# New duration constants for the planner of a decoder layer with a selective scan and a routed mixture of experts

## The chip, the cores and the metric

The kernel runs on one core of a Trainium2 chip. The metric is device time in microseconds. The core has five engines that work side by side, each taking its own instructions strictly in the order in which the program holds them: TensorE (PE, matmuls), VectorE (DVE), ScalarE (ACT), GpSimd (POOL) and SyncE (SP), which here only issues DMA transfers.

## What is computed

One decoder layer on x of shape 4 x 512 x 512 (batch, positions, width): a state-space block with a scan over positions, a quantized two-layer product in place of cross attention, and a mixture of 16 experts of which each token takes two, beside a shared expert. Cut to what matters:

```python
x = x + attn(layernorm(x))      # the scan block
x = x + xattn(layernorm(x), fside, ctx)
x = x + ffn(layernorm(x))

# attn: xz = in_proj(h); x = silu(conv1d(x)); dt, Bc, Cc = x_proj(x)
# delta = softplus(dt_proj(dt) + bias); A = -exp(A_log)
def step(h, inputs):
    d_t, B_t, C_t, u_t = inputs
    h = h * exp(d_t * A) + (d_t * u_t) * B_t      # 1024 channels x 16 states
    return h, (h * C_t).sum(states)
# y = (ys + u * D) * silu(z); out_proj(y)

# xattn: int8-like: both operands scaled by column and row maxima, rounded
#        to -127..127, multiplied, scaled back; silu(gate) * up between two such
# ffn:   softmax routing, top 2 of 16 experts (width 128), weighted sum,
#        plus sigmoid(x @ g) * shared expert (width 512)
```

## The kernel before

The scan runs on VectorE for one batch element b after the other, and in it for eight channel blocks c of 128 channels (NC = 8). A channel block takes eight slots (NU = 8), so that there are 4 x 8 x 8 = 256 slots. In a slot (`scan_batch`) ScalarE computes two exponentials `da` of 128 x 512 for the next slot (`unit_inputs`, L709) and GpSimd the product `bu` (L711); VectorE runs the scan of 128 x 1024 in place on `da` (`unit_scan`, L718) and multiplies the result by C into `h` (`unit_out`, L724), of which there are five buffers. Twice in eight slots PE sums the states of four such `h` into the PSUM tile `py` (`state_sums`, L736: 16 quarter-array matmuls for the eight slots), and VectorE multiplies the sum by the gate (`gated`, L758).

Everything else is placed beside these slots, in pieces called steps. Each kind of work is a Python generator that yields what its next step waits for:

- `delta(b, c)`: the step size of channel block c, one matmul, five ACT operations with one change of table, four POOL operations; its result is replicated by DMA (`spread`, tile `rep`) and feeds `da` and `bu`. It is wanted one channel block later; if it is late, `end` forces its steps out.
- `front(b)`, b = 1 to 3: layernorm, 64 matmuls of in_proj (L446, four of 512 columns to a product), convolution, gate, x_proj.
- `back(b)`: out_proj (L791), two quantized products, and the mixture's front: routing and the shared expert. Backs 0 to 2 run beside the scans of the next batch; the last comes after the scans.
- `experts` for group 0 (batches 0 and 1; beside the last scan batch) and group 1 (batches 2 and 3; after the scans): sorting of the tokens, then tiles of 128 tokens with weights fetched by an indirect DMA (L1223), tokens by another (L1467), transposes, the products L1498 and L1513, and at the end the fetch and weighted sum of the rows (L1261, L1271).

What places a step is `Pace`, an estimate of when each engine is free and each tile written. For each instruction already in the program, `take` adds a cost to its engine's clock: a fixed part (FIXED) and a part per element (EACH) for DVE, ACT and POOL, a product of columns for PE (`product`), and a fixed part for a DMA issue. A written tile is ready for others HOP = 120 ns after that. Nothing of this runs on the chip; it decides only the order in which instructions stand in each engine's program.

Three times in a slot `more` asks the waiting steps in turn, and `clear` says yes if every engine of the step is at most BEHIND past VectorE's clock (0 DVE, 1500 ACT, 500 POOL, 5000 PE, 4000 SP, in ns) and its inputs are ready at most SLACK past it (200 DVE, 700 ACT, -300 POOL, 3500 PE, 500 SP). For engines other than DVE the slot's own coming work (3500, 1200 or 0 ns, by the place in the slot) is added. Steps behind a planned count (`due`) are given 100 ns more for each step that they are late. After the scans `run` takes the step that the estimate has ready first.

The three PSUM banks bank_a, bank_b and bank_g serve all steps beside the scan; after it there are five more.

Of the kernel before, what the change touches and what calls it, by code (L numbers as in the profile page):

```python
# [8 lines left out]
F32 = mybir.dt.float32  # L9
# [21 lines left out]
CH = 32  # L31
# [15 lines left out]
PE, ACT, POOL, SP = "PE", "Activation", "Pool", "SP"  # L47
# [15 lines left out]
class Bank:  # L63
# [9 lines left out]
    def take(self, shape, dtype=F32):  # L73
        pool, name = self.names.pop(0)
        t = pool.tile(shape, dtype, name=name, tag=name, bufs=1)
        self.held[name_of(t)] = pool, name
        return t
# [7 lines left out]
    def staged(self, items, product, *stages, freed=1):  # L85

        gap = [nothing] * (self.depth - freed)
        return staged(items, product, *gap, *stages, every=1 if gap or self.depth == freed else freed, bank=self)
# [44 lines left out]
class Pace:  # L133

    FIXED = {"DVE": 60, "Activation": 220, "Pool": 130, "PE": 30, "SP": 60}
    EACH = {"DVE": 1.1, "Activation": 0.92, "Pool": 2.2}
    HOP = 120
    TABLES = {"Exp": 0, "Tanh": 0, "Silu": 1, "Ln": 2}  # L140

# [4 lines left out]
    def __init__(self, nc):  # L146
        self.nc, self.seen, self.table, self.queue = nc, 0, None, 0
        self.rest = 0
        self.engine = dict.fromkeys(self.FIXED, 0)
        self.written, self.read = {}, {}  # L150
# [6 lines left out]
    def take(self, ins):  # L157
        outs = [x for x in ins.outs if hasattr(x, "bass_ap")]
        ins_ = [x for x in ins.ins if hasattr(x, "bass_ap")]
        e = str(ins.engine).rsplit(".", 1)[-1]  # L160
        if not outs or e not in self.engine:
            return
        n = 1
        for _, size in list(outs[0].ap)[1:]:
            n *= size
        kind = type(ins).__name__
        keys, outs_ = [self.key(x) for x in ins_], [self.key(x) for x in outs]
        start = max([self.engine[e]] + [self.written.get(k, 0) for k in keys])
        if e != "SP":
            start = max([start] + [max(self.written.get(k, 0), self.read.get(k, 0)) for k in outs_])  # L170
        if "DMA" in kind:
            end = start + (950 if e == "Pool" else self.FIXED[e])
            size = 1
            for _, x in outs[0].ap:
                size *= x
            self.queue = max(self.queue, end) + size * 4 / 220
            self.engine[e], done = end, max(self.queue, end + 1000) + 1000
        else:
            if e == "PE":
                cost = 40 + self.product(n / 4 if outs[0].ap[0][1] == CH else n, ins_[0].dtype == F32)  # L180
            else:
                cost = self.FIXED[e] + n * self.EACH[e] * (2 if getattr(ins, "is_tensor_tensor_scan", False) else 1)
            if e == "Activation" and kind == "InstActivation":
                table = self.TABLES.get(str(ins.func).rsplit(".", 1)[-1], self.table)
                if table != self.table:
                    cost += 1280
                    self.table = table
            self.engine[e] = start + cost
            done = self.engine[e] + self.HOP
        for k in keys:  # L190
            self.read[k] = max(self.read.get(k, 0), done)
        for k in outs_:
            self.written[k] = done

    def product(self, cols, full):

        return max(2.3 * cols, 300) if full else max(0.5 * cols, 120)

    def update(self):
        ins = self.nc.cur_bb.bb.instructions  # L200
# [69 lines left out]
class Kernel:  # L270
# [271 lines left out]
    def first_front(self, sb, bank):  # L542
# [54 lines left out]
        for _ in staged(range(NC), product, conv, silu, nothing, sums):  # L597
            pass
# [1168 lines left out]
```

## Time and profile before

| | us |
|---|---|
| median of 3 runs | 1646.77 (1646.59 to 1649.17) |
| the profiled execution | 1661.86 |
| its span, first to last instruction | 1659.9 |
| scan stages, about | 90 to 1335 |
| idle of ACT before da, for h | 229.4 |
| idle of POOL before bu, for da | 140.2 |
| longest wait of VectorE for bu | 27.4 |

The profile is one execution taken by the hardware profiler. A row of the groups gives source line, engine and operation, output and inputs with shapes, the count, then busy us in all and the mean ns of one, then the idle time of the engine just before and what ended it. ACT's and POOL's long waits above are for buffers that VectorE gives back: these engines are ahead of it there. An fp32 matmul leaves two records on PE, so counts of matmuls there are twice the program's.

The time of PE depends on the clock that it is granted. The page gives it in forty slices of the span, in tenths of full speed:

```
PEclk9978888768877887899978897987777999868995
```

### The profile page before, as it was taken

How to read it: one execution, taken by the hardware profiler on the slowest of the kernel's cores; microseconds unless marked ns; L12 is line 12 of the kernel's file. 1: busy time of each engine (PE TensorE's matmuls, PEld its weight loads, DVE VectorE, ACT ScalarE, POOL GpSimd, SP SyncE). 2: the span in 40 equal slices, each digit the busy share in tenths (PEclk: the TensorE clock that was granted, in tenths of full speed). 3: DMA queues.
4: the chain of work that ended last, by engine and by line, in shares of the span. 5: the costliest groups of instructions: out<-in, count | busy, mean ns of one | idle time of the engine just before them, and what ended most of it. 6: DMA issues, size and time to landing. Idle time of an engine off the chain costs nothing. (4 is left out here: it accounts for less than half of the span.)

```text
span 1659.9 us, 15722 instructions
## 1 busy us (share of the span) xinstructions
PE 1207.7 (73%) x4552; PEld 584.8 (35%) x4552; DVE 1193.2 (72%) x1250; ACT 941.3 (57%) x1592; POOL 1130.7 (68%) x940
## 2 busy tenths in 40 slices
PE   6848777557866767898867885866667899668980
PEld 2213222112332323333423432343424347434760
DVE  4369999898867888778878898877778934352312
ACT  3376786755757778555787762567575414520330
POOL 1178999886767988676787874777788644126464
PEclk9978888768877887899978897987777999868995
DMA  5575655675233556665335658555567464168956
GB/s 192 154 162 126 141 110 111 130 189 110 74 90 78 135 120 163 161 203 143 78 84 127 172 137 293 138 158 133 130 184 204 120 260 146 65 230 292 342 213 216
DMA packets 109658, 262.22 MB, mean 158 GB/s; under 512 B 16192, under 2 KB 20416, under 8 KB 109504
## 3 DMA queue, kind: packets, MB, share of 16 engines
q1 hardware_dynamic: 93120, 204.50, 47.4%
q0 software_dynamic: 16448, 56.65, 9.8%
q8 instruction: 40, 0.66, 0.2%
q14 instruction: 50, 0.41, 0.1%
HBM read 168.55 MB, written 45.88 MB: 129 GB/s over the span
## 5 line engine op out<-in xcount | busy, mean ns | idle before, releaser
L711 POOL TENSOR_TENSOR bu<-bc,rep 128x1024 f32<-128x1024 f32 x256 | 602.2, 2358 | 169.8 <-DVE da L718 140.2
L718 DVE TENSOR_TENSOR_SCAN da<-da,bu 128x1024 f32<-128x1024 f32 x256 | 586.2, 2290 | 105.2 <-POOL bu L711 74.4
L709 ACT ACTIVATE da<-rep,a_sb 128x512 f32<-128x512 f32 x512 | 352.7, 690 | 261.2 <-DVE h L724 229.4
L724 DVE TENSOR_TENSOR h<-da,bc 128x1024 f32<-128x1024 f32 x256 | 312.3, 1220 | 19.6 <-PE py L736 9.2
L736 PE MATMUL py<-h,sel 128*32 128x512 f32 x1024 | 166.1, 687 | 50.2 <-DVE h L724 50.1
L1223 POOL DMA_INDIRECT wx<-in_wexp,wrow x62 | 63.0, 1016 | 79.9 <-PE bank L1513 22.9
L446 PE MATMUL bank_g<-xnT,win 128*128 128x512 f32 x192 | 100.2, 670 | 8.6 <-ACT tap L498 6.0
L502 POOL TENSOR_TENSOR u<-u,tap 128x511 f32<-128x511 f32 (+2 forms) x72 | 91.3, 1268 | 18.1 <-ACT tap L498 15.9
L446 PE MATMUL bank_b<-xnT,win 128*128 128x512 f32 x160 | 82.1, 661 | 24.6 <-ACT sp_r L669 15.2
L736 PEld LDWEIGHTS py<-h,sel 128*32 128x32 f32 x1024 | 31.1, 119 | 164.4 <-issue 83.3
L1467 POOL DMA_INDIRECT xs<-xn_d,tok x62 | 64.3, 1038 | 20.9 <-issue 19.2
L446 PE MATMUL bank_a<-xnT,win 128*128 128x512 f32 x128 | 63.2, 640 | 3.0 <-DVE gz L411 2.4
L446 PEld LDWEIGHTS bank_g<-xnT,win 128*128 128x128 f32 x192 | 40.5, 219 | 63.0 <-issue 51.2
L446 PEld LDWEIGHTS bank_b<-xnT,win 128*128 128x128 f32 x160 | 32.9, 213 | 72.9 <-issue 38.5
L680 POOL TENSOR_TENSOR sp_e<-sp_e,dd 128x512 f32<-128x512 f32 x32 | 40.7, 1272 | 26.2 <-ACT dd L675 26.1
L1261 POOL DMA_INDIRECT yg<-y_d,pos x32 | 33.3, 1041 | 23.9 <-DMA y_d<-ys 9.5
L1504 ACT ACTIVATE hs<-bank 128x128 f32<-128x128 f32 x24 | 6.6, 276 | 67.5 <-PE bank L1498 36.5
L1271 DVE SCALAR_TENSOR_TENSOR xr<-yg,topw,xr 128x512 f32<-128x512 f32 x32 | 23.7, 750 | 28.8 <-DMA yg<-y_d,pos 28.5
L791 PE MATMUL bank_b<-wout,u 128*128 128x512 f32 x64 | 36.1, 724 | 10.7 <-ACT tap L498 6.2
L1498 PE MATMUL bank<-xT,wx 128*128 128x128 f32 x352 | 43.1, 276 | 0.6 <-issue 0.6
L1498 PEld LDWEIGHTS bank<-xT,wx 128*128 128x128 f32 x352 | 41.3, 192 | 4.3 <-issue 3.5
L411 DVE SCALAR_TENSOR_TENSOR hs<-hs,bank 128x128 f32<-128x128 f32 x24 | 6.8, 284 | 50.1 <-ACT hs L1504 35.7
(422 smaller groups left out, 2439.4 us busy)
## 6 DMA issues: line engine op xcount, KB each, us to landing
rep<-dd SPq DMA_DIRECT2D x128, 512.0 KB
win<-in_win SPq DMA_DIRECT2D x64, 256.0 KB
x<-xr SPq DMA_DIRECT2D x48, 256.0 KB
xr<-x SPq DMA_DIRECT2D x48, 256.0 KB
y_d<-ys SPq DMA_DIRECT2D x48, 256.0 KB
bc<-rows_d SPq DMA_DIRECT2D x32, 256.0 KB
gz_d<-gz SPq DMA_DIRECT2D x32, 256.0 KB
gzl<-gz_d SPq DMA_DIRECT2D x32, 256.0 KB
```

Of the source, the lines that this page charges most:

```text
L446: nc.tensor.matmul(pj, win[:, k, :], xnT[:, k, :], start=(k == 0), stop=(k == NK - 1))
L502: nc.gpsimd.tensor_add(u[:, j:], u[:, j:], v[j][:, j:])
L680: nc.gpsimd.tensor_sub(e, e, du)
L709: nc.scalar.activation(da[:, i, :], rep[:, i, 0, :], AF.Exp, scale=self.a_sb[:, q, g : g + 1])
L711: nc.gpsimd.tensor_mul(bu, st["bc"][0, g].unsqueeze(1).to_broadcast([P, NP, L]), rep[:, :, 1, :])
L718: self.nc.vector.tensor_tensor_scan(daf, daf, buf, 0.0, ALU.mult, ALU.add)
L724: self.nc.vector.tensor_mul(h, st["da"].pop((c, n)), st["bc"][1, g].unsqueeze(1).to_broadcast([P, NP, L]))
L736: nc.tensor.matmul(py[q * CH : (q + 1) * CH, :], self.sel, st["h"][c, g, q // NP][:, q % NP, :], start=False, stop=(g == NG - 1),)
L791: nc.tensor.matmul(po[t], st["u"][c][:, t * P : (t + 1) * P], wout[c], start=(c == part[0]), stop=(c == part[-1]),)
L1223: nc.gpsimd.indirect_dma_start(out=ws[s], out_offset=None, in_=self.wexp, in_offset=bass.IndirectOffsetOnAxis(ap=wrow[:, s : s + 1], axis= ...
L1467: nc.gpsimd.indirect_dma_start(out=xs[s], out_offset=None, in_=xn_d, in_offset=bass.IndirectOffsetOnAxis(ap=tok[:, s : s + 1], axis=0), bo ...
L1498: nc.tensor.matmul(ph[:, i, :], w[:, o : o + P], xT[:, k, :], start=(k == 0), stop=(k == NK - 1))
```

## The change

The constants of the estimate are replaced: those of VectorE, ScalarE, GpSimd and PE, the cost of a GpSimd DMA issue, and the 40 ns that were added to each matmul. HOP, the table load, the DMA queue's rate, SLACK, BEHIND and the due times stay as they are. The diff:

```diff
-    FIXED = {"DVE": 60, "Activation": 220, "Pool": 130, "PE": 30, "SP": 60}
-    EACH = {"DVE": 1.1, "Activation": 0.92, "Pool": 2.2}
+    FIXED = {"DVE": 150, "Activation": 190, "Pool": 180, "PE": 0, "SP": 60}
+    EACH = {"DVE": 1.044, "Activation": 0.9, "Pool": 2.13}
     HOP = 120
...
         if "DMA" in kind:
-            end = start + (950 if e == "Pool" else self.FIXED[e])
+            end = start + (1030 if e == "Pool" else self.FIXED[e])
...
             if e == "PE":
-                cost = 40 + self.product(n / 4 if outs[0].ap[0][1] == CH else n, ins_[0].dtype == F32)
+                cost = self.product(n / 4 if outs[0].ap[0][1] == CH else n, ins_[0].dtype == F32)
...
     def product(self, cols, full):
-        return max(2.3 * cols, 300) if full else max(0.5 * cols, 120)
+        return max(1.8 * cols, 240) if full else max(0.6 * cols, 110)
```

`full` is true for fp32 operands. `n / 4` is used for the state sums, whose four quarter-array matmuls of 32 output rows count as 128 columns each. For scans the part per element counts twice.

## The prediction

> **What bounds the kernel now.** I read the page's busy shares first, then busy time by stage, then the costliest groups, then the waits of VectorE, and the timeline where a number had to be taken apart.
>
> ```profile
> PE 1207.7 (73%) x4552; PEld 584.8 (35%) x4552; DVE 1193.2 (72%) x1250; ACT 941.3 (57%) x1592; POOL 1130.7 (68%) x940
> ```
>
> No engine is full over the span. The stages say more (columns: stretch, its length, then busy us of PE, weight loads, DVE, ACT, POOL, granted clock, DMA share, GB/s):
>
> ```profile
> 90.00:360.00 270.00, 184.75 (x536) 62.18 (x536) 244.26 (x164) 196.37 (x310) 238.93 (x168) 0.82 0.59 128
> 360.00:670.00 310.00, 218.85 (x776) 99.33 (x776) 252.73 (x226) 221.08 (x372) 246.59 (x198) 0.82 0.50 121
> 670.00:1000.00 330.00, 272.45 (x920) 119.68 (x919) 273.91 (x252) 218.16 (x360) 251.62 (x188) 0.89 0.55 138
> 1000.00:1335.00 335.00, 232.83 (x996) 122.75 (x995) 273.57 (x290) 187.61 (x323) 237.40 (x198) 0.82 0.59 167
> 1335.00:1660.00 325.00, 237.58 (x1197) 157.26 (x1195) 112.93 (x275) 88.44 (x187) 143.55 (x161) 0.85 0.63 224
> ```
>
> From 90 to 1335 us the scan runs, 256 slots of it. VectorE is the backbone: 244.3 of 270 us in the first batch (90%), then 252.7 of 310, 273.9 of 330 and 273.6 of 335 (82% together). The sum of its idle time there is 1245 - 1044.5 = 200.5 us. Behind the scan lie 325 us in which PE is the busiest at 73%. A slot's own work:
>
> ```profile
> L711 POOL TENSOR_TENSOR bu<-bc,rep 128x1024 f32<-128x1024 f32 x256 | 602.2, 2358 | 169.8 <-DVE da L718 140.2
> L718 DVE TENSOR_TENSOR_SCAN da<-da,bu 128x1024 f32<-128x1024 f32 x256 | 586.2, 2290 | 105.2 <-POOL bu L711 74.4
> L709 ACT ACTIVATE da<-rep,a_sb 128x512 f32<-128x512 f32 x512 | 352.7, 690 | 261.2 <-DVE h L724 229.4
> L724 DVE TENSOR_TENSOR h<-da,bc 128x1024 f32<-128x1024 f32 x256 | 312.3, 1220 | 19.6 <-PE py L736 9.2
> ```
>
> VectorE needs 2290 + 1220 = 3510 ns a slot; measured is 1245 / 256 = 4.86 us. The difference is the work placed beside the scan and the idle time. Who is waited for by VectorE from 90 to 1335 us (total us, times, longest):
>
> ```profile
> DVE da L718 <- POOL bu L711: 74.4, 29, 27.4
> DVE da L718 <- ACT da L709: 29.4, 17, 4.4
> DVE u L758 <- PE py L736: 12.2, 4, 8.5
> DVE h L724 <- PE py L736: 9.2, 3, 5.3
> ```
>
> 41.0 us of the first line fall before 360, the 27.4 at the scan's start. The waits on PE are few.
>
> **The change, part by part.** No instruction is added or removed. The constants only move the planner's clocks, and with them the place of each step. So the cost is the order's cost, bounded from the estimates' errors.
>
> *VectorE and GpSimd.* By the formula a scan goes from 60 + 2.2 x 1024 = 2313 to 2288 (row 2290), h from 1186 to 1219 (row 1220), bu from 2383 to 2361 (row 2358). A slot's VectorE estimate goes from 3499 to 3507 ns: nothing. GpSimd's own DMA issues go from 950 to 1030 ns (rows 1016 to 1041): 28 issues beside the scan (62 + 62 in all, 48 + 48 of them after 1335) x 80 ns = 2.2 us of estimate, nothing. SP's constant stays; its issues move with their steps, and SP mostly waits for their data, so no queue there is costlier.
>
> *ScalarE.* 512 elements go from 691 to 651 ns; the row of da says 690, while small copies take 620 to 680. Two da a slot become 80 ns cheaper in the plan than their row. Since da waits for h in each slot, the error does not add up: 0 to +0.1 us a slot on the few slots where ACT is last (17 waits): at most 2 us.
>
> *PE.* This is the change. A 512-column fp32 matmul goes from 40 + 1178 = 1218 to 922 ns; a 128-column one, and each of the state sums' quarter-array ones, from 340 to 240. The load that the planner sees for eight slots of the middle batches: state sums 16 x 340, one skip and one delta matmul: 7.9 us, now 5.7; a front's ten 512-column matmuls 12.2, now 9.2; an eighth of a back (80 of 512 columns, 168 of 128, some bf16) 20.7, now 15.5. Sum 40.8 before, 30.4 after. Measured, eight slots take (1000 - 360) / 128 x 8 = 40 us. So the old planner held PE for full, and spread its steps; the new one sees it at three quarters, and admits them sooner. Real matmuls:
>
> ```profile
> 548.98 6.68 PE L446 MATMUL bank_g<-xnT,win 128*128 128x512 f32 x8 [5.41 <-ACT tap L498]
> 557.71 1.92 PE L736 MATMUL py<-h,sel 128*32 128x512 f32 x16
> 559.56 3.70 PE L446 MATMUL bank_b<-xnT,win 128*128 128x512 f32 x8
> ```
>
> Eight records are one product of four matmuls (each fp32 matmul leaves two). After a pause of 5.41 us it takes 6.68 us, warm 3.70: 1.67 and 0.925 us a matmul. The new constant is the warm one. **A rule against it**: the Trainium skill ("TensorE: Matmul & The Clock Gate", Part 1) says the array drops to half clock after an idle window of about 3.4 us and needs as long a busy one to recover. The row agrees: 6.68 against 3.70, and the granted clock of the scan is 0.82 to 0.89, which is a third of its time at half: (1 - 0.84) / 0.5. Weighted so, a matmul is 0.67 x 0.925 + 0.33 x 1.67 = 1.17 us at worst, my estimate, or 922 / 0.84 = 1.10. By the old constant the plan is 4 to 11% long; by the new, 16 to 21% short. By the rule's mean the eight-slot load would be 30.4 / 0.84 = 36 us, between the two.
>
> What does that cost? The planner admits a PE step while PE's clock is under 5 us (plus up to 3.5) past VectorE's; these tolerances stay. Behind an admitted product stand, on PE's in-order queue, the state sums, and behind these the five h buffers and the py bank that VectorE needs next. The sums are issued at the start of a slot and the first h buffer is wanted some 1.7 slots later, 1.7 x 4.86 = 8 us. A backlog planned at 5 us is on the mean 4.5 to 4.8 today and 6.0 to 6.3 with the new constants; with the 3.5 us besides, about 10, past the cover. Batches 1 to 3 hold 24 x 2 = 48 state sums; a third fall in half clock, 16. Bounds: 0 (the cover holds, as for 45 of 48 today) to 16 x 3 us = 48. I take 8, near today's rows (9.2 + 12.2), since steps rarely fill the tolerance.
>
> Besides, VectorE's small operations that read PE's result are placed once the plan has it ready (200 ns slack). Some 46 a back (4 out_proj sums, 22 in the two quantized products, the rest in the mixture's front) and 3 a channel block: 3 x 46 + 24 x 3 = 210. Each now goes up to 0.3 us earlier (1218 - 922) for each matmul before it; where it was waited for anyway nothing is lost. Bounds: -10 (results truly ready that were left lying) to 210 x 0.3 = 63; I take 14, a third of them at 0.2.
>
> *What it gives.* Steps once held for PE go sooner. A place where that was late:
>
> ```profile
> 472.40 2.30 DVE L718 TENSOR_TENSOR_SCAN da<-da,bu 128x1024 f32<-128x1024 f32 x1 [11.64 <-POOL bu L711]
> 474.60 0.67 DVE L411 SCALAR_TENSOR_TENSOR u<-bank_b,u 128x512 f32<-128x512 f32 x1
> 475.19 0.68 DVE L951 TENSOR_REDUCE wsc<-bank_a 128x1 f32<-128x512 f32 x1
> ```
>
> There the delta of the next block came late, its spread was still landing, and VectorE stood 11.64 us. Such waits for POOL and ACT between 360 and 1335 sum to 103.8 - 41.0 - 5.0 = 58 us (5.0 is ACT's share before 360). Bounds 0 to -58; I take -12, one such stall.
>
> *A second rule.* The two last lines start 0.59 us apart, though each lasts 0.67. "Perfetto Trace Analysis" (Optimizing Scalar/DVE Operations) says why: a profiled duration holds a write acknowledgement that the next instruction overlaps. The old formula gave 60 + 563 = 623 for this shape, the new 684. By the row's spacing the old one is nearer: 420 such operations (932 of VectorE in the scan stages less 512) x 0.08 = 34 us of invented VectorE time, 2.7% of 1245. It makes the plan's "now" late and so the other engines' tolerances looser: the same direction, inside the bounds above.
>
> *Behind the scan* the step that is ready first by the estimate is taken. The order of the last back and the tiles can move, by an amount no row tells: -10 to +10 (3% of 325), 0 taken.
>
> Sum: +8 + 14 - 12 + 0 = **+10 us**. The profiled execution took 1661.9 us (span 1659.9 and 2.0 around it), 0.9% above the median of 1646.8; differences of 10 us need no scaling. Forecast **1657 us**.
>
> **The rivals.**
>
> *Faster: POOL and ACT are no longer booked into time that does not exist.* A plan bound by PE (40.8 us and its waits) stretches its own clock, so that VectorE, POOL and ACT seem to have room; with PE right, it spaces their steps by the real period. For it: where PE was light, in the first batch, VectorE was 90% busy. Half of the 58 us goes: -29. And the tail shrinks: expert tiles leave 16 records each on L1498, 736 in all and 528 after 1335, so 46 tiles, 13 of them beside the scan and, with 23 a group, 10 of the first left over. Three more moved, at about 3.8 us of PE, times PE's 73%: -8. It gives 1647 - 37 = 1610. It decides once the plan admits the late deltas' steps without queueing over the sums. Against it: the waits are scattered, and the first batch has no backs.
>
> *Much slower: chains fall behind in slots.* A shorter planned slot means that a step waiting for ACT or POOL becomes ready more slots later; fewer tiles run beside the scan, and the due-time term forces late steps onto busy queues. Five tiles fewer: +19, and the forecast's +10: 1676. Against it: PE's part of the chains shortens too.
>
> *No effect*: forced points (late deltas, due steps) decide the order, or the gains cancel: 1647.
>
> **How the numbers follow.** Forecast 0.44 (own range 1650 to 1668), faster 0.36, much slower 0.13, no effect 0.07. Within 0.2% is about what a measurement of this kernel can tell from no change (3.3 us). Faster 0.36, same 0.07, slower 0.57. The range runs from 1598 (-58 and a few tiles cut by a third) to 1700 (+48 + 14 less the gain): both signs hold most of the chance.
>
> **What would show it.** Right: waits of h and of the gating (L758) on PE py rise above 21 us, the small readers' waits on PE grow, POOL waits fall a little, the scan still ends near 1335 to 1350. Wrong: the scan's VectorE share rises above 86% with PE waits unchanged (rival one), or more than 33 tiles behind the scan (rival two). An unchanged order of the engines would undo all of it.

## The result, and the profile after

The changed kernel takes **1674.4 us** (four runs, 1673.0 to 1676.0) against 1646.8 before: ratio 1.0166, with a 95% interval of 1.0144 to 1.0189. That is 28 us slower. The direction was forecast and the time lies in the stated range, but the forecast was +10 us.

The one profiled execution that the prediction was worked from took 1661.9 us, 15 us above the median of its kernel. The same program profiled again (run e1_before_again) gave 1642.9 us of span and 1646.9 us median; it stands for "before" in what follows. Busy shares after, from the page:

```profile
PE 1208.3 (72%) x4552; PEld 590.7 (35%) x4552; DVE 1195.7 (71%) x1250; ACT 943.3 (56%) x1592; POOL 1128.9 (67%) x940
```

The work is the same. Busy time by stage, first for the kernel before (profiled again), then for the changed one. The stages run from the first scan to the first scan of the next batch, the fourth to the last scan, the fifth to the end; columns as in the prediction.

```profile
89.40:350.20 260.80, 176.79 (x524) 59.49 (x524) 237.82 (x159) 192.95 (x304) 234.86 (x166) 0.81 0.59 128
350.20:667.50 317.30, 224.45 (x788) 99.65 (x788) 260.85 (x233) 225.33 (x379) 252.29 (x202) 0.83 0.51 124
667.50:991.30 323.80, 267.34 (x914) 118.26 (x915) 270.53 (x249) 216.11 (x358) 249.11 (x186) 0.90 0.55 138
991.30:1328.50 337.20, 234.93 (x999) 127.56 (x998) 275.06 (x290) 188.46 (x324) 238.59 (x199) 0.81 0.59 167
1328.50:1642.90 314.40, 237.63 (x1197) 160.03 (x1195) 113.54 (x275) 89.16 (x187) 144.05 (x161) 0.83 0.65 232
```

```profile
89.70:363.50 273.80, 188.69 (x524) 62.09 (x524) 239.33 (x160) 192.58 (x304) 234.60 (x166) 0.76 0.55 121
363.50:676.30 312.80, 239.28 (x836) 107.34 (x840) 264.19 (x239) 225.87 (x381) 253.33 (x202) 0.85 0.54 132
676.30:1013.10 336.80, 263.00 (x898) 116.84 (x892) 269.88 (x247) 214.35 (x354) 245.58 (x185) 0.89 0.51 130
1013.10:1374.80 361.70, 253.19 (x1129) 144.82 (x1126) 280.17 (x302) 195.01 (x340) 248.97 (x209) 0.84 0.61 176
1374.80:1673.30 298.50, 205.12 (x1041) 136.90 (x1039) 106.71 (x260) 85.32 (x172) 133.06 (x151) 0.83 0.61 216
```

The second column is what to read. The scan lasts 1239.1 us before and 1285.1 after: +13.0, -4.5, +13.0 and +24.5 by batch, +46 in all. Behind it 314.4 became 298.5: -16. The sum is the +30 between the two profiles.

VectorE's longest waits from the first to the last scan, before (again) and after, with us, times and longest:

```profile
DVE da L718 <- POOL bu L711: 73.9, 28, 27.2
DVE da L718 <- ACT da L709: 29.1, 17, 4.4
DVE u L758 <- PE py L736: 10.7, 5, 6.9
DVE h L724 <- PE py L736: 6.3, 2, 4.5
DVE xsc L1005 <- PE bank_b L940: 6.2, 5, 2.5
```

```profile
DVE da L718 <- POOL bu L711: 61.6, 23, 27.3
DVE da L718 <- ACT da L709: 41.6, 27, 5.2
DVE xn L1122 <- PE bank_b L1099: 17.4, 6, 7.0
DVE xn L1122 <- PE bank_a L1099: 11.0, 5, 4.7
DVE xsc L1005 <- PE bank_a L940: 10.9, 5, 8.5
DVE h L724 <- PE py L736: 10.7, 5, 3.9
```

L1122, the shared expert's product read from PSUM, stands in the second list with 28.4 us; before it was 5.4. Summed over all lines and batches, VectorE's waits went from 208 to 245 us: on PE 67 to 97, on ACT 47 to 65, on POOL 93 to 78, on a DMA 0 to 5. It was also busy 9 us longer there (1044.3 to 1053.6), since more steps stand beside the scan. 37 + 9 = 46.

How such a wait looks, in the changed kernel's last batch, first VectorE, then PE:

```profile
1310.49 2.29 DVE L718 TENSOR_TENSOR_SCAN da<-da,bu 128x1024 f32<-128x1024 f32 x1
1317.49 0.69 DVE L1122 SCALAR_TENSOR_TENSOR xn<-xn,bank_a 128x512 f32<-128x512 f32 x1 [4.71 <-PE bank_a L1099]
1318.10 0.68 DVE L411 SCALAR_TENSOR_TENSOR xn<-xn,bank_b 128x512 f32<-128x512 f32 x1
1318.70 1.22 DVE L724 TENSOR_TENSOR h<-da,bc 128x1024 f32<-128x1024 f32 x1
```

```profile
1309.91 3.67 PE L1107 MATMUL bank_b<-xnT,ws 128*128 128x512 f32 x8 [3.27 <-DMA ws<-in_wexp]
1313.42 0.60 PE L400 MATMUL bank_g<-ident,xs 128*128 128x128 f32 x4
1313.86 3.60 PE L1099 MATMUL bank_a<-xnT,ws 128*128 128x512 f32 x8
```

The scan ends at 1312.8. VectorE's order has L1122 next; PE had waited 3.27 us for weights and finishes its product at 1317.5. Behind L1122 stands the h that ends the slot, though its own input is there. So the larger part of this wait came with the weights' DMA; in all, PE waited 18 us for these weights (tile ws) during the scan, 11 before. From the 241st scan to the last it is 89.1 us here and 69.6 before.

### The profile page after: what moved, and what is told of

It reads as the page before. It is cut to its first block, busy times and chain, and to the rows that moved or that the text cites. A ratio compares the mean times of both kernels' runs of the same rounds, so it can differ in the third digit from the quotient of the medians.

```text
span 1673.3 us, 15705 instructions
## 1 busy us (share of the span) xinstructions
PE 1208.3 (72%) x4552; PEld 590.7 (35%) x4552; DVE 1195.7 (71%) x1250; ACT 943.3 (56%) x1592; POOL 1128.9 (67%) x940
## 5 line engine op out<-in xcount | busy, mean ns | idle before, releaser
L724 DVE TENSOR_TENSOR h<-da,bc 128x1024 f32<-128x1024 f32 x256 | 312.5, 1221 | 21.5 <-PE py L736 10.7
L736 PEld LDWEIGHTS py<-h,sel 128*32 128x32 f32 x1024 | 30.2, 115 | 200.4 <-DVE h L724 127.7
L446 PE MATMUL bank_a<-xnT,win 128*128 128x512 f32 x168 | 91.3, 694 | 2.9 <-DVE gz L411 1.1
L446 PE MATMUL bank_g<-xnT,win 128*128 128x512 f32 x152 | 75.5, 643 | 2.6 <-ACT tap L498 1.9
L446 PEld LDWEIGHTS bank_a<-xnT,win 128*128 128x128 f32 x168 | 36.9, 228 | 54.5 <-issue 46.2
L446 PEld LDWEIGHTS bank_g<-xnT,win 128*128 128x128 f32 x152 | 30.8, 208 | 46.3 <-issue 38.6
L1498 PE MATMUL bank_g<-xT,wx 128*128 128x128 f32 x208 | 32.3, 321 | 13.3 <-ACT xT L1489 7.3
L684 POOL TENSOR_TENSOR dd<-sp_e,sp_w 128x512 f32<-128x512 f32 x32 | 40.6, 1267 | 1.6 <-ACT sp_w L678 0.6
L686 POOL TENSOR_TENSOR dd<-dd,u 128x512 f32<-128x512 f32 x32 | 40.6, 1270 | 1.4
L682 POOL TENSOR_TENSOR sp_e<-sp_e,sp_r 128x512 f32<-128x512 f32 x32 | 40.6, 1269 | 1.4
```

The source lines that it names most:

```text
L446: nc.tensor.matmul(pj, win[:, k, :], xnT[:, k, :], start=(k == 0), stop=(k == NK - 1))
L682: nc.gpsimd.tensor_add(e, e, r)
L724: self.nc.vector.tensor_mul(h, st["da"].pop((c, n)), st["bc"][1, g].unsqueeze(1).to_broadcast([P, NP, L]))
L736: nc.tensor.matmul(py[q * CH : (q + 1) * CH, :], self.sel, st["h"][c, g, q // NP][:, q % NP, :], start=False, stop=(g == NG - 1),)
```

## The experiments

Each is timed against the kernel before, side by side on the same chip, and shown as a ratio with its interval. "Scan" is the time from the first scan to the last, "three" the part of it that the first three batches take, "behind" what follows the last scan, "PE" VectorE's waits on PE during the scan, "tiles" the expert tiles begun beside it, all from the run's own profile.

| run | ratio | scan, us | three, us | behind, us | PE, us | tiles |
|---|---|---|---|---|---|---|
| e1_before_again | 1.0002 [0.9989, 1.0015] | 1239 | 902 | 314 | 67 | 13 |
| the change | 1.0166 [1.0144, 1.0189] | 1285 | 923 | 298 | 97 | 18 |
| e1_pe_only | 1.0201 [1.0176, 1.0226] | 1295 | 941 | 297 | 105 | 17 |
| e1_rest_only | 0.9917 [0.9899, 0.9934] | 1236 | 901 | 309 | 63 | 15 |
| e1_hop125 | 1.0029 [1.0011, 1.0046] | 1249 | 910 | 314 | 87 | 13 |
| e2_tol | 1.0160 [1.0126, 1.0195] | 1288 | 921 | 304 | 107 | 17 |
| e2_new_to_192 | 1.0099 [1.0077, 1.0120] | 1242 | 917 | 339 | 73 | 10 |
| e2_new_from_192 | 1.0198 [1.0173, 1.0223] | 1287 | 906 | 314 | 106 | 19 |
| e2_hold | 1.0232 [1.0205, 1.0259] | 1273 | 920 | 329 | 94 | 13 |
| e3_late | 0.9975 [0.9956, 0.9995] | 1245 | 905 | 325 | 68 | 15 |
| e3_early | 1.0362 [1.0327, 1.0397] | 1317 | 962 | 317 | 116 | 17 |
| e3_mean | 1.0238 [1.0202, 1.0273] | 1300 | 952 | 310 | 116 | 18 |
| e3_slow | 1.0365 [1.0329, 1.0400] | 1257 | 922 | 372 | 64 | 12 |
| e4_margin | 1.0086 [1.0053, 1.0119] | 1288 | 932 | 299 | 124 | 17 |
| e4_after_hop115 | 1.0343 [1.0303, 1.0384] | 1320 | 942 | 311 | 154 | 17 |
| e4_rest_hop115 | 1.0033 [1.0017, 1.0049] | 1245 | 909 | 328 | 79 | 14 |
| e4_rest_plus | 1.0171 [1.0128, 1.0215] | 1245 | 908 | 356 | 75 | 14 |
| e5_large_old | 1.0119 [1.0088, 1.0149] | 1282 | 929 | 290 | 104 | 17 |
| e5_small_old | 0.9882 [0.9854, 0.9909] | 1254 | 928 | 287 | 106 | 13 |

**Which half of the change?** Before with one half of the constants, with nothing, and with another signal time.

> The kernel before, unedited, profiled once more. Every theory expects 1646 to 1650 us timed. Its first profile was 15 us above its own median; if that was one odd execution, this profile's run is within 5 us of 1647, and the stages that lengthened can be read from its windows. If profiled executions of this kernel are long as such, it is near 1660 again.

> The kernel before with only PE's constants of the change (no 40 ns, 1.8 ns a column with a floor of 240, 0.6 with a floor of 110). Theory 1, PE is overbooked beside the scan: nearly the whole loss is here, 1667 to 1680 us, with more than 13 expert tiles beside the last scan batch and the last scan after 1355. Theory 2, any re-ordering of this plan costs: slower too, but no more than the other half of the constants, 1655 to 1665. Rival, PE's true durations help and the others hurt: at or below 1640.

```diff
-                cost = 40 + self.product(...)
+                cost = self.product(...)
-        return max(2.3 * cols, 300) if full else max(0.5 * cols, 120)
+        return max(1.8 * cols, 240) if full else max(0.6 * cols, 110)
```

> The kernel before with the change's constants of VectorE, ScalarE and GpSimd, and PE's old ones. Theory 1: within 8 us of 1647. Theory 2 (any re-ordering costs): 1655 to 1680, as much as PE's half. Rival, the others hurt: 1665 or more.

```diff
-    FIXED = {"DVE": 60, "Activation": 220, "Pool": 130, "PE": 30, "SP": 60}
-    EACH = {"DVE": 1.1, "Activation": 0.92, "Pool": 2.2}
+    FIXED = {"DVE": 150, "Activation": 190, "Pool": 180, "PE": 0, "SP": 60}
+    EACH = {"DVE": 1.044, "Activation": 0.9, "Pool": 2.13}
-            end = start + (950 if e == "Pool" else self.FIXED[e])
+            end = start + (1030 if e == "Pool" else self.FIXED[e])
```

> The kernel before with the estimate's signal time at 125 ns in place of 120: an order as different as chance makes it, with no duration truer or falser. Theory 1: within 8 us of 1647. Theory 2: 1655 to 1680, like the change.

```diff
-    HOP = 120
+    HOP = 125
```

PE's half alone gives 1.0201, as much as the whole within the intervals; the other half 0.9917, a gain. The loss is PE's. "Any re-ordering costs" is not borne out: an order changed by nothing but 5 ns of signal time gives 1.0029, the other half's a gain.

**Is it the tolerance, the batch, or the work pulled in?** These are edits of the changed kernel.

> The changed kernel with PE's two tolerances cut by the ratio of the constants, 922/1218 = 0.76: BEHIND 5000 to 3800, SLACK 3500 to 2650 ns. If the loss is a backlog admitted by tolerances that stayed in nanoseconds (the prediction's step), the time falls to 1635 to 1655. If it is the length of the plan, PE's load being taken for three quarters of what it is, whatever the tolerance, it stays at 1665 to 1685.

```diff
-    SLACK = {..., "PE": 3500, ...}
-    BEHIND = {..., "PE": 5000, ...}
+    SLACK = {..., "PE": 2650, ...}
+    BEHIND = {..., "PE": 3800, ...}
```

> The changed kernel's constants up to slot 192 (fronts, backs 0 and 1), then the old ones for the last scan batch and behind it. If the loss is spread over all batches: 1655 to 1665. If it comes from the last batch, where expert tiles and the last back's out_proj enter beside the scan: 1640 to 1652.

> The reverse: the old constants up to slot 192, the change's from there. Spread loss: 1655 to 1665. Loss of the last batch: 1665 to 1680, the whole of it.

```diff
+            if self.slot == 192:
+                self.pace.use(False)
```

(`use` puts all constants of the change, or all the old ones, in force. The second run begins with the old ones and has `use(True)` here.)

> The changed kernel with two kinds of work kept behind the scan: no expert tile after the 13th begins beside it, and the last back's out_proj waits for its end. Theory, work pulled beside the scan lengthens it while behind it that work was hidden by the last back's chain: last scan before 1350 and 1640 to 1660 us. If the loss lies in how the other steps stand: 1670 or more.

```diff
-            while started < loaded and len(going) < bank.depth:
+            while started < loaded and len(going) < bank.depth and (started < 13 or "scans" in self.done):
...
-                    yield PE, *wout, lambda: ("gated", b, part[-1]) in self.done
+                    yield PE, *wout, lambda: ("gated", b, part[-1]) in self.done and "scans" in self.done
...
+            if not going:
+                yield lambda: "scans" in self.done
+                continue
...
         self.finish(B - 1, 1)
+        self.done.add("scans")
```

The tolerance, the prediction's own mechanism for the queue, is not borne out: with it cut in proportion the ratio stays at 1.016. The two halves in time give 1.0099 and 1.0198; they don't add up to 1.0166, but neither is free, so the loss isn't the last batch's alone. The column "three" says it more closely, since several runs have the same constants up to slot 192: with the old ones the first three batches take 902 to 908 us (e1_before_again, e2_new_from_192, and the profile that the prediction read), with the change's 917 to 923 (the change, e2_new_to_192, e2_hold).

Holding work back made it worse. Its last scan batch and what follows:

```profile
1011.70:1364.70 353.00, 234.85 (x990) 125.46 (x986) 275.88 (x290) 189.00 (x326) 240.31 (x191) 0.80 0.57 165
1364.70:1693.40 328.70, 238.68 (x1178) 160.80 (x1178) 110.90 (x272) 90.46 (x186) 142.01 (x168) 0.84 0.59 212
```

Against the change the batch is 8.7 us shorter (361.7 to 353.0) and the rest 30.2 longer (298.5 to 328.7). So the work pulled beside the scan was worth its place, and that theory falls too. From the last scan to the last routing matmul (L1157) are 143 us before and 116 after the change, where the last back's out_proj begins 18 us before the last scan and not 9 after it. The 16 us that the end gained go with this.

**PE as busy, or PE's results as ready?** Here PE's estimate is split in two clocks.

> The changed kernel with PE's estimate split in two: PE counts as busy by the new, short durations, while its results count as ready by the old, long ones. Theory R, the loss comes from results promised too early, so that their readers stand at the head of VectorE's and ScalarE's queues: the loss is gone, ratio 0.985 to 1.000. Theory Q, it comes from PE being admitted more work: ratio 1.012 to 1.022 as with the change.

> The reverse split: PE counts as busy by the old, long durations, its results as ready by the new, short ones. Theory R: the loss stays, 1.012 to 1.025. Theory Q: it is gone, 0.985 to 1.002.

```diff
+                cost = self.product(cols, full)
+                self.shadow = max(self.shadow, begin) + self.slower(cols, full)
...
-            done = self.engine[e] + self.HOP
+            done = (self.shadow if e == "PE" else self.engine[e]) + self.HOP
```

(`begin` is when the operands are ready; `slower` the old formula with its 40 ns. For e3_early the two formulas change places.)

> The changed kernel with PE's durations at what the trace gives on the mean over both clocks, 2.2 ns a column, floor 290 (bf16 0.73, floor 135), in place of 1.8 and 240. If the fault of the new constants is that they hold for the full clock alone: ratio 0.985 to 0.998. If the old ones were good for being longer than the truth: between the two, 1.003 to 1.012.

> The changed kernel with PE's durations half as long again as the change's: 2.8 ns a column, floor 380 (bf16 0.93, floor 170), above the old ones. If any slack is good: 0.985 or lower. If there is a best value near the true mean: 1.000 or more, since steps come too late and work is left behind the scan.

```diff
-        return max(1.8 * cols, 240) if full else max(0.6 * cols, 110)
+        return max(2.2 * cols, 290) if full else max(0.73 * cols, 135)    # e3_mean
+        return max(2.8 * cols, 380) if full else max(0.93 * cols, 170)    # e3_slow
```

e3_early speaks for the results: promised by the new durations, they keep the loss, and more, although PE counts as busy by the old (1.0362, waits on PE 116 us). e3_late looks like the other side of this (0.9975, 68 us) but does not test it. The planner lets a matmul wait for the promised result of the one before it on the same tile, so there PE's clock follows the long durations after all, and the plan is almost e1_rest_only's: by their traces, all but about one in a hundred of VectorE's instructions stand in the same order. (That these two give 0.9917 and 0.9975 also shows how far ratios from different groups of runs can lie apart.) e3_mean, half or more of the way back to the old durations, is worse than the change. e3_slow shows the other end: fewest waits on PE (64), a scan of 1257 us, and 372 us behind it, because the steps come too late (12 tiles).

**A margin, luck, or one kind of matmul?**

> The changed kernel, all its durations kept, with one addition: a result of PE counts as ready 1000 ns later for the readers on other engines (not for PE's own next matmul on the same tile). That is about what four matmuls lost in the change (4 x 296 ns). Theory R, the old long durations were good as a margin on PE's results: ratio 0.985 to 1.002 and VectorE's waits on PE in the scan stages fall from 97 to below 75 us. If the old durations were good for another reason, or by chance of order: 1.010 or more.

```diff
-        start = max([self.engine[e]] + [self.written.get(k, 0) for k in keys])
+        written = {**self.written, **self.own} if e == "PE" else self.written
+        start = max([self.engine[e]] + [written.get(k, 0) for k in keys])
...
         for k in outs_:
+            self.own.pop(k, None)
+            if e == "PE":
+                self.own[k] = done
-            self.written[k] = done
+            self.written[k] = done + (1000 if e == "PE" else 0)
```

(`own` holds what PE itself waits for.)

> The changed kernel with the signal time at 115 ns in place of 120: another order of the same plan. If the change's loss belongs to its durations, it stays: 1.010 to 1.025. If it is the luck of one order: anything from 0.99 to 1.03, and a value at or below 1.003 would show it.

> The new durations of VectorE, ScalarE and GpSimd with PE's old ones, and the signal time at 115 ns. If the gain of that half (0.992) belongs to its durations: 0.988 to 0.998. If it was luck: 1.000 or more.

```diff
-    HOP = 120
+    HOP = 115
```

> The same half with PE's old durations made 8% longer (2.5 ns a column, floor 325, and the 40 ns). A broad best around the old values gives 0.988 to 1.002; a best that lies in one order alone gives 1.010 or more; results that are promised later still take VectorE's waits on PE in the scan stages to 65 us or below in any case.

```diff
-        return max(2.3 * cols, 300) if full else max(0.5 * cols, 120)
+        return max(2.5 * cols, 325) if full else max(0.54 * cols, 130)
```

The margin fails in its own measure, and that speaks against theory R: at 1.0086 half the loss is gone, yet the waits on PE are the second longest of all. Three of its lines (five source lines were added, so L1127 is the change's L1122):

```profile
DVE xn L1127 <- PE bank_a L1104: 24.0, 7, 9.3
DVE h L729 <- PE py L741: 19.5, 6, 9.0
DVE u L763 <- PE py L741: 10.0, 5, 3.6
```

The two runs at 115 ns give the size of luck: 5 ns move the changed kernel by 1.8% (1.0166 to 1.0343) and the other half by 1.2% (0.9917 to 1.0033). So the change's loss stays a loss with the other time, and the other half's gain is not certain. A difference of 1 to 2% between two single orders can be luck. PE's durations 8% over the old ones already cost 1.7% against before, and that behind the scan (356 us).

> The changed kernel with the old 1218 ns for PE's 512-column fp32 matmuls only; the short ones keep 240 ns. By the planner's load for eight slots 22 large matmuls x 296 ns are 6.5 of the 10.4 us that the change took away. If PE's load as the plan sees it is what matters: most of the loss goes, ratio 0.995 to 1.008, VectorE's waits on PE in the scan stages 65 to 85 us. If it is the promise of the short matmuls, whose results are read at once (scaled weights, maxima): 1.012 or more.

> The reverse: 340 ns for fp32 matmuls of up to 128 columns (state sums included), 922 for the large ones. Load theory: 37 x 100 ns are 3.7 of 10.4 us, so most of the loss stays, 1.008 to 1.022, waits on PE above 85 us. Short-promise theory: 0.990 to 1.003.

```diff
-        return max(1.8 * cols, 240) if full else max(0.6 * cols, 110)
+        return (40 + 2.3 * cols if cols > 128 else 240) if full else max(0.6 * cols, 110)    # e5_large_old
+        return (1.8 * cols if cols > 128 else 340) if full else max(0.6 * cols, 110)         # e5_small_old
```

The load theory is not borne out: the old value for the long matmuls leaves 1.0119, although they make up most of the planned load. With the old 340 ns for the short ones alone, and everything else as in the change, the kernel takes 1629.9 us (1623.9 to 1632.5): ratio 0.9882, **faster than both**. Its last batch and its end:

```profile
1016.90:1342.80 325.90, 232.01 (x1019) 124.06 (x1016) 276.47 (x292) 188.28 (x325) 238.80 (x199) 0.82 0.61 175
1342.80:1629.50 286.70, 212.86 (x1151) 147.81 (x1149) 109.46 (x270) 89.29 (x187) 143.39 (x161) 0.85 0.69 248
```

The last batch is 35.8 us shorter than the change's, and the end 11.8. It keeps the early start of the last out_proj (at 1325, before the last scan; from the last scan to the last routing 117 us, as the change), with only 13 tiles beside the scan. But its first three batches are not mended: 928 us, against 923 with the change and 902 before. What it gains lies in the last batch and behind it. Nor is the gain in the waits on PE (106 us against 97): the waits on ACT fell, from 65 us to 36.

Sorted afterwards by the duration planned for short fp32 matmuls, the runs fall apart in their total time: with 340 ns six between 0.988 and 1.003 (before, e1_hop125, e1_rest_only, e3_late, e4_rest_hop115, e5_small_old); with 240 or 290, nine between 1.009 and 1.036; above 340, two that are slow behind the scan. e4_margin counts here by its 240 ns, though it promises the results 1000 ns later. The gap between the groups is small beside the luck inside them, and in all of the six but e5_small_old the long matmuls have their old duration too. That one edit, which changes nothing else, moves the time by 2.8%, more than any change of signal time did; no second order of it was run.

The first three batches sort the runs otherwise, and there both mixed runs are on the slow side. Where all of PE's results are promised by the old durations up to slot 192, or by ones 8% longer, they take 901 to 910 us; in every other run, e5_small_old and e5_large_old among them, 917 to 962. So neither kind of matmul alone accounts for the loss there.

## Why the prediction was wrong

It said slower for the right engine, at about a third of the size. Term by term, against the profiles:

- *VectorE's waits on PE, +22 (8 for the state sums, 14 for the small readers).* Measured +30, but not in these parts. The waits behind the state sums (L724 and L758 on py) went from 17.0 to 12.5 us: nothing was lost there, and cutting the tolerance changed nothing (e2_tol). The readers of other results went from 50 to 85, 2.5 times the 14: the term was of the right kind and too small.
- *Stalls recovered, -12.* POOL's share came as forecast, 93 to 78.
- *ScalarE, "at most 2 us".* **This is the step that failed.** VectorE's waits on ACT rose by 18 us, 23 of it in the first batch (3.0 to 25.7, where only fronts and deltas stand beside the scan) and given back in part later. I priced da by its own duration and put at nothing what stands before da on ScalarE's queue: operations that read PE's results. ScalarE's own waits on PE in the scan went from 103 to 174 us. Two of its lines in the first batch, before (again) and after, and one such wait after the change:

```profile
ACT rows L536 <- PE bank_a L455: 2.8, 1, 2.8
ACT gz L510 <- PE bank_b L446: 2.4, 1, 2.4
```

```profile
ACT gz L510 <- PE bank_a L446: 8.6, 2, 6.2
ACT rows L536 <- PE bank_b L455: 5.2, 1, 5.2
```

```profile
288.18 0.57 ACT L536 COPY rows<-bank_b 32x512 f32<-32x512 f32 x1 [5.23 <-PE bank_b L455]
289.86 1.40 ACT L709 ACTIVATE da<-rep,a_sb 128x512 f32<-128x512 f32 x2
291.35 2.30 DVE L718 TENSOR_TENSOR_SCAN da<-da,bu 128x1024 f32<-128x1024 f32 x1 [5.23 <-ACT da L709]
```

  ScalarE stood 5.23 us for x_proj's product, the da behind it came late, and VectorE stood as long. If each of VectorE's waits on ACT is put down to what ScalarE itself had last waited for (0.1 us or more), PE's share is 19 of 47 us before and 53 of 65 after. ScalarE's constants are not needed for it: e1_pe_only, which keeps them, has 68 us of waits on ACT in the scan and 187 of ScalarE on PE; e1_rest_only has 53 and 115. In the first batch the other half adds to it (e1_pe_only 12.5 us, e1_rest_only 18); ScalarE's constants by themselves weren't tried. So the small readers' mechanism, for which the prediction allowed on VectorE alone, works through ScalarE's queue as well.
- *More work beside the scan, 0.* Measured 9 us of VectorE time, and a late DMA 5.
- *Behind the scan, 0.* Measured -16, outside the bounds of 10, with the earlier out_proj (where it is held back, in e2_hold, the end takes 329 us).

22 to 30, -12 to -16, 0 in the sum to 18, 0 to 14 and 0 to -16 make the step from +10 to +30, the difference of the two profiles.

The reasoning behind the PE part had a fault as well: "by the new, 16 to 21% short". The planner lets a matmul wait for the previous one on the same tile, and adds the signal time of 120 ns to each result. So a matmul within a product is planned at 922 + 120 = 1042 ns now, 1338 before. Measured before the change (again), records within in_proj products in the scan start 501 ns apart on the mean, two to a matmul: 1002 ns, and not the 1.10 to 1.17 us that I had from weighting the two clocks. The new plan is 4% long on the mean for long matmuls, and the old one a third too long. For short ones the new plan has 360 ns and the old 460; those of L940 take 298. The change did make PE's estimate truer, and PE's half of it cost 2.0%; I had the sign by a wrong account of why, so that it was in part luck. e3_mean, meant to hold the mean of both clocks, has 1126 ns for 512 columns and so the same fault; it did not mend the loss.

The term from VectorE's small operations ("the same direction") shows no loss either: e1_rest_only has their longer durations and is not slower. By the prediction's own figures the change adds 684 - 623 = 61 ns to each, 26 us for the 420, not 34.

Rival "faster" falls: POOL's waits shrank by 16 us, ACT's grew. Rival "much slower" has the time nearly right (1676) by the wrong way: 18 tiles stood beside the scan, not five fewer. The rise of L724's and L758's waits above 21 us, named as what would show it right, did not come; the small readers' did.

What stays open: which results of PE, promised too early, cost the time. e3_early says that the promise matters and e4_margin does not bear it out. Why 340 ns for short matmuls that take about 300 give the fastest kernel is not known, nor for which of them (state sums, scaled products, transposes, routing), nor whether it is more than one lucky order. Its waits add up to 217 us against the change's 245, and the waits on ACT make the difference, not those on PE. No run separated the kinds.

## What to carry to other kernels

A truer duration in a planner need not make a faster kernel: here PE's truer ones cost 2.0%. Change one engine's, and one size of operation, at a time. When a result is expected too early, look for its readers on every engine, and for what stands behind them in the queue. Measure the luck of an order with an edit that means nothing (5 ns of signal time moved this kernel by 0.3 to 1.8%) before a gain of 1% is believed. And price a re-ordering by the whole ledger of the backbone's waits, by engine that it waits on, with what becomes of the work behind it.

## What was not expected of the hardware

The same program took 1646.5 to 1647.9 us (medians) in some groups of runs and 1660.7 to 1663.9 in others, 0.9 to 1.1% apart, for a reason that the runs do not show: both were measured on one chip (number 10 of the record), with granted clocks of 0.84 to 0.85. The profile that the prediction read was 15 us above the median that it was compared with, more than the whole forecast; only ratios within one group of runs could be used. A product of four 512-column fp32 matmuls took 3.60 to 3.70 us after steady work and 6.68 after a pause of 5.41, and the first batch's granted clock was 0.76 in the changed order against 0.81, for the same 524 records.
